# Eight PSUM banks dealt out anew in a kernel of two attentions and a mixture of experts

## The chip, the cores and the metric

The kernel runs on one core of one Trainium2 chip. The metric is the device time of one execution in microseconds (us). A core has five engines that run side by side, each through a queue of its own in fixed order: TensorE (PE, matmuls; its weight loads are shown apart as PEld), VectorE (DVE), ScalarE (ACT), GpSimd (POOL) and SyncE (SP), which here only issues DMAs. Matmuls write to PSUM, which has eight banks of 128 partitions x 512 fp32 numbers; DVE and ACT read the results from there.

## The reference, cut to what matters

The input x has 16 sequences of 256 tokens with 128 channels, all fp32. Four blocks follow each other, each with a layernorm ahead of it and its result added to x:

```
x = x + attention_a(layernorm(x))   # 16 heads of 8, in blocks of 64 tokens
x = x + ffn(layernorm(x))           # 8 experts, hidden 512, the best 2 per token
x = x + attention_b(layernorm(x))   # 16 heads of 8, across the 16 sequences, with a bias
x = x + ffn(layernorm(x))           # the same experts again

scores = einsum(q, k) * scale (+ bias);  attn = softmax(scores);  out = einsum(attn, v)
g = x @ Wg[e];  u = x @ Wu[e];  h = silu(g) * u;  y = (h @ Wd[e]) / sqrt(12)
out = y of the two chosen experts, weighted by the softmax of their two logits
```

## The kernel before, in words

The tokens are cut into four quarters (64 positions of all 16 sequences), each quarter into two halves, each half into four groups of 128 tokens. x stays in SBUF.

**First attention** (`prepare_a`, `attention_a`, layer 0). For each half `prepare_a` normalizes, transposes (product lnp), and makes keys and queries (products k and q). Queries are copied out of their bank by four ACT instructions (line 313). Then for each group: a product v for the values (line 339), two score tiles sc, one for each block of 64 tokens (line 396); DVE takes the maximum over keys (line 404) and subtracts it (line 405), which is the last reading of the score bank; ACT takes exp of both tiles in one instruction (line 410); PE transposes them in two products t (line 415), which ACT copies (line 419); PE multiplies with the values into the product o (line 426), which DVE divides (lines 356, 358).

**Second attention** (`normal_b`, `prepare_b`, `attention_b`, `finish_b`, layer 1). It has the same steps, with one score tile for each group (line 503), read once by DVE, which adds the bias (line 510); the output is transposed once more (product ot, line 481) and projected (product y_B, line 560).

**Router** (`router`, `tile_tables`). After each quarter it normalizes again, computes logits (product lg, line 585) and ranks (line 648 waits for a copy by POOL), and writes the rows by indirect DMA, sorted by expert. It runs beside the next quarter.

**Experts** (`experts`). Each of the two layers has 39 tiles of 256 rows. A tile is fetched with its expert's three weights by SP's DMAs, turned (product xt, line 875, copied by ACT in line 877), and worked on in two pairs of hidden chunks. A pair computes gate g and up u into one bank each (line 933, 128 x 512); ACT takes tanh of g (line 938), DVE multiplies with g again (line 939, the last reading of g) and with u (line 941, the only reading of u). The down product acc collects both pairs (line 883); ACT copies it (line 891), PE turns it back (product y, line 894), ACT scales it (line 899) and POOL writes the rows out by indirect DMA (line 906). The down matmuls of one pair are written behind gate and up of the next.

**Order.** `weave` and `run` at the end write the order of the work: the generators of attention, preparation, router and expert units are stepped in fixed ratios. No expert work stands beside the first three quarters of the first attention; about half of what layer 0's first lists hold is put beside the fourth, and the later units run beside the second attention. A planner in the framework then fixes each engine's queue, starting from that order, and says which bank each tile gets; on the chip an instruction waits for the last reader of the tile that held its bank before.

**PSUM.** Four pools hold the eight banks: `ps_gu` (tag gu) has three, for g and u; `ps_acc` one, for acc; `ps_sc` (tag sc) two, for the scores of both attentions (lines 393 and 500); `ps_mm` (tag mm) two, for every product called small here (function `psum`: lnp, k, q, v, t, o, xt, y, ot, y_B, lg, rank, count).

Of the kernel before, what the change touches and what calls it, by code (L numbers as in the profile page):

```python
# [10 lines left out]
F32 = mybir.dt.float32  # L11
# [6 lines left out]
PSUM = bass.MemoryType.PSUM  # L18

P = 128  # L20
# [90 lines left out]
def hybrid_kernel(  # L111
# [24 lines left out]
    p6 = ctx.enter_context(tc.tile_pool(name="p6", bufs=6))  # L136
    p3 = ctx.enter_context(tc.tile_pool(name="p3", bufs=3))
    dram = ctx.enter_context(tc.tile_pool(name="dram", bufs=1, space=bass.MemoryType.DRAM))
    ps_gu = ctx.enter_context(tc.tile_pool(name="ps_gu", bufs=3, space=PSUM))
    ps_acc = ctx.enter_context(tc.tile_pool(name="ps_acc", bufs=1, space=PSUM))  # L140
    ps_sc = ctx.enter_context(tc.tile_pool(name="ps_sc", bufs=2, space=PSUM))
    ps_mm = ctx.enter_context(tc.tile_pool(name="ps_mm", bufs=2, space=PSUM))


    xq = [const.tile([P, NG, C], F32, name=f"xq{q}") for q in range(NQ)]
# [110 lines left out]
    def psum(name):  # L256
        return ps_mm.tile([P, 512], F32, tag="mm", name=name)
# [95 lines left out]
    def divided(o, name):  # L353
        o = o.rearrange("p (h d) -> p h d", d=D + 1)
        rec = p2.tile([P, H], F32, tag="rec", name=f"rec_{name}")
        nc.vector.reciprocal(rec, o[:, :, D])
        att = p2.tile([P, H, D], F32, tag="att", name=f"att_{name}")
        att_last[0] = nc.vector.tensor_tensor(  # L358
            att, o[:, :, 0:D], rec.unsqueeze(2).to_broadcast([P, H, D]), ALU.mult
        ).ins  # L360
        return att.rearrange("p h d -> p (h d)")
# [20 lines left out]
    def attention_a(q, half):  # L382
        lnT, qT, kx = ready.pop((q, half))
        for g in range(4 * half, 4 * half + 4):
            n = f"A{q}_{g}"
            vt = va[g % 2]
            values(vt, lnT, g % 4, 2, wv_sb, n)
            yield


            ex = p2.tile([P, 2, 8, BS], F32, tag="ex", name=f"ex_{n}")
            for b in range(2):
                sc = ps_sc.tile([P, 512], F32, tag="sc", name=f"sc_{n}_{b}")
                blk = 2 * (g % 4) + b
                for v in range(2):
                    nc.tensor.matmul(  # L396
                        sc[:, v * 4 * BS : (v + 1) * 4 * BS],
                        lhsT=qT[:, blk, 2 * v : 2 * v + 2, :].rearrange("p r k -> p (r k)"),
                        rhs=kx[:, :, blk * BS : (blk + 1) * BS],
                        start=True, stop=True,  # L400
                    )
                sc3 = sc.rearrange("p (h k) -> p h k", k=BS)
                mx = p3.tile([P, 16], F32, tag="mx", name=f"mx_{n}_{b}")
                nc.vector.tensor_reduce(mx[:, 0:8], sc3, AX.X, ALU.max)  # L404
                beat[0] = nc.vector.tensor_tensor(  # L405
                    ex[:, b], sc3, mx[:, 0:8].unsqueeze(2).to_broadcast([P, 8, BS]),
                    ALU.subtract,
                ).ins
                yield
            beat[0] = nc.scalar.activation(ex, ex, AF.Exp).ins  # L410
            eT = p2.tile([P, 2, 4, P], F32, tag="eT", name=f"eT_{n}")
            for b in range(2):
                pt = psum(f"t_{n}_{b}")
                for i in range(4):
                    nc.tensor.transpose(  # L415
                        pt[:, i * P : (i + 1) * P],
                        ex[:, b, 2 * i : 2 * i + 2, :].rearrange("p h k -> p (h k)"), ident,
                    )
                nc.scalar.copy(eT[:, b].rearrange("p a b -> p (a b)"), pt)  # L419
                yield  # L420
            po = psum(f"o_{n}")
            for b in range(2):
                for i in range(8):

                    u, v = i // 2 % 2, i // 4
                    nc.tensor.matmul(  # L426
                        po[b * BS : (b + 1) * BS, i * 18 : (i + 1) * 18],
                        lhsT=eT[:, b, 2 * v + i % 2, u * BS : (u + 1) * BS],
                        rhs=vt[:, b, 2 * i : 2 * i + 2, :].rearrange("p h d -> p (h d)"),
                        start=True, stop=True,  # L430
                    )
            att = divided(po[:, 0 : H * (D + 1)], n)
            beat[0] = att_last[0]
            nc.gpsimd.tensor_tensor(att, att, bv_bc, ALU.add)  # L434
            nc.gpsimd.tensor_tensor(xq[q][:, g, :], xq[q][:, g, :], att, ALU.add)
            yield
# [36 lines left out]
    def attention_b(q, half):  # L473
        xt, qT, kx = ready.pop((q, half))
        if half == 0:
            outs[q] = p1.tile([P, S, BS], F32, tag="oT", name=f"oT_{q}")
        oT = outs[q]

        def turn(g, att):
            pot = psum(f"ot_B{q}_{g}")  # L480
            nc.tensor.transpose(pot[:, 0:P], att, ident)
            nc.scalar.activation(
                oT.rearrange("c s t -> c t s")[:, 8 * g : 8 * g + 8, :],
                pot[:, 0:P].rearrange("c (t s) -> c t s", s=S),
                AF.Identity, bias=b_sb[:, B_IV : B_IV + 1],
            )

        pending = None
        for dg in range(2 * half, 2 * half + 2):
            for gg in range(2):  # L490
                g = 2 * dg + gg
                values(vb[gg], xt, g % 4, 4, wi_sb[:, 2 * P : 3 * P], f"B{q}_{g}")
                yield


            ex = p2.tile([P, 2, H, 32], F32, tag="ex", name=f"ex_B{q}_{dg}")
            for gg in range(2):
                g = 2 * dg + gg
                n = f"B{q}_{dg}_{gg}"
                sc = ps_sc.tile([P, 512], F32, tag="sc", name=f"sc_{n}")  # L500
                for j in range(4):
                    blk = 4 * (g % 4) + j
                    nc.tensor.matmul(  # L503
                        sc[:, j * P : (j + 1) * P],
                        lhsT=qT[:, blk].rearrange("p r k -> p (r k)"),
                        rhs=kx[:, :, blk * 32 : (blk + 1) * 32],
                        start=True, stop=True,
                    )
                sb = p2.tile([P, H, 32], F32, tag="sb", name=f"sb_{n}")
                nc.vector.tensor_tensor(  # L510
                    sb, sc.rearrange("p (h k) -> p h k", k=32),
                    pair_bias.unsqueeze(1).to_broadcast([P, H, 32]), ALU.add,
                )
                yield
                mx = p3.tile([P, 16], F32, tag="mx", name=f"mx_{n}")
                nc.vector.tensor_reduce(mx, sb, AX.X, ALU.max)
                beat[0] = nc.vector.tensor_tensor(
                    ex[:, gg], sb, mx.unsqueeze(2).to_broadcast([P, H, 32]), ALU.subtract
                ).ins
                yield  # L520
            nc.scalar.activation(ex, ex, AF.Exp)
            for gg in range(2):
                g = 2 * dg + gg
                n = f"B{q}_{g}"
                pt = psum(f"t_{n}")
                for j in range(4):
                    nc.tensor.transpose(  # L527
                        pt[:, j * P : (j + 1) * P],
                        ex[:, gg, 4 * j : 4 * j + 4, :].rearrange("p h k -> p (h k)"),
                        ident,  # L530
                    )
                eT = p2.tile([P, 2, 4, P], F32, tag="eT", name=f"eT_{n}")
                nc.scalar.copy(eT[:, 0].rearrange("p a b -> p (a b)"), pt)
                yield
                if pending is not None:
                    turn(*pending)
                po = psum(f"o_{n}")
                for j in range(4):
                    for r in range(4):
                        nc.tensor.matmul(  # L540
                            po[32 * j : 32 * (j + 1), r * 36 : (r + 1) * 36],
                            lhsT=eT[:, 0, j, 32 * r : 32 * (r + 1)],
                            rhs=vb[gg][:, j, 4 * r : 4 * r + 4, :].rearrange(
                                "p h d -> p (h d)"
                            ),
                            start=True, stop=True,
                        )
                pending = g, divided(po[:, 0 : H * (D + 1)], n)
                beat[0] = att_last[0]
                yield  # L550
        turn(*pending)
        yield
# [476 lines left out]
    for layer in range(2):  # L1029
# [10 lines left out]
        for q in range(NQ):  # L1040
            for half in range(2):
# [20 lines left out]
                if layer == 1 and half == 1:  # L1062
                    finish_b(q)
                    if q == NQ - 2:
                        n = BEGIN_B - 3
# [53 lines left out]
```

## Time and profile before

| | |
|---|---|
| three runs, us | 1083.53, 1084.24, 1073.32 (median 1083.53) |
| profiled execution, us | 1007.37 |
| its span from the first to the last instruction, us | 1005.3 |
| mean granted TensorE clock in it | 0.923 |
| PE, PEld, DVE, ACT, POOL busy, share of the span | 88%, 72%, 62%, 39%, 37% |
| HBM traffic | 106 GB/s over the span |
| first attention alone / with experts | 20 to 233 us / 233 to 345 us |
| experts of layer 0 alone | 345 to 455 us |
| second attention with experts | 455 to 830 us |
| experts of layer 1 alone, and the end | 830 to 1005 us |

The profile is one execution recorded by the hardware. Its page begins with the busy time of each engine, then cuts the span into 40 equal slices (a digit is the busy share in tenths; PEclk is the clock that PE was granted, in tenths of full speed). A row of waits reads: the instruction that stood, what released it, us in total, times, longest. A row of the timeline reads: start, duration, engine, line, operation, what is written from what, shapes, count, and in brackets the idle time of the engine ahead of it and its releaser. A row of a stage table reads: stretch, its length, busy us of PE, PEld, DVE, ACT and POOL with their counts of instructions, PE's clock, the share of the DMA engines, GB/s. Releasers are inferred from semaphore events. Ends of matmuls are modelled, so a busy PE is not PE at its peak.

### The profile page before, as it was taken

How to read it: one execution, taken by the hardware profiler on the slowest of the kernel's cores; microseconds unless marked ns; L12 is line 12 of the kernel's file. 1: busy time of each engine (PE TensorE's matmuls, PEld its weight loads, DVE VectorE, ACT ScalarE, POOL GpSimd, SP SyncE). 2: the span in 40 equal slices, each digit the busy share in tenths (PEclk: the TensorE clock that was granted, in tenths of full speed). 3: DMA queues.
4: the chain of work that ended last, by engine and by line, in shares of the span. 5: the costliest groups of instructions: out<-in, count | busy, mean ns of one | idle time of the engine just before them, and what ended most of it. 6: DMA issues, size and time to landing. Idle time of an engine off the chain costs nothing.

```text
span 1005.3 us, 17682 instructions
## 1 busy us (share of the span) xinstructions
PE 880.1 (88%) x5992; PEld 723.8 (72%) x5992; DVE 623.4 (62%) x1741; ACT 395.9 (39%) x773; POOL 371.3 (37%) x460
## 2 busy tenths in 40 slices
PE   3988698888999999989987989797988999998993
PEld 1776577665878888877766777585767787886882
DVE  5666555665576685559657665674867685555542
ACT  2443333233353434335543345352534333443431
POOL 2112442261165375337001362163516457332322
PEclk9998776798999999999978699799999999999997
DMA  7000000013133476675110122025403456668762
GB/s 192 19 2 1 17 29 1 9 41 105 44 109 112 126 207 208 191 229 169 44 64 22 43 87 67 20 81 174 127 10 110 138 148 193 198 181 271 225 192 83
DMA packets 104922, 107.69 MB, mean 107 GB/s; under 512 B 10688, under 2 KB 80320, under 8 KB 104832
## 3 DMA queue, kind: packets, MB, share of 16 engines
q1 hardware_dynamic: 95024, 87.36, 29.8%
q0 software_dynamic: 9088, 18.89, 5.4%
q8 instruction: 48, 0.79, 0.3%
q10 hardware_dynamic: 720, 0.30, 0.1%
q14 instruction: 42, 0.34, 0.1%
HBM read 83.38 MB, written 23.13 MB: 106 GB/s over the span
## 4 chain that ended last, share of the span: by engine, by line
PE 65%; DVE 13%; DMA 6%; ACT 5%; POOL 5%; issue 4%; SPq 1%; ACTq 0%; POOLq 0%; DVEq 0%
PE g L933 11%; PE u L933 10%; PE acc L883 10%; PE o_A L426 5%; PE sc_A L396 4%; PE v_B L339 4%; PE o_B L540 3%; PE t_A L415 3%; PE sc_B L503 2%; DMA back<-results 2%; DMA results<-yo,to 2%; PE t_B L527 2%; DMA xin<-sorted_in 2%; PE lg_F L585 2%; POOL sorted_in L680 2%
## 5 line engine op out<-in xcount | busy, mean ns | idle before, releaser
L906 POOL DMA_INDIRECT results<-yo,to x156 | 153.3, 982 | 235.8 <-ACT yo L899 203.5
L883 PE MATMUL acc<-h,w 128*128 128x256 f32 x624 | 167.0, 388 | 2.8 <-DVE h L941 2.5
L933 PE MATMUL u<-xT,w 128*128 128x256 f32 x624 | 163.8, 384 | 5.4 <-DVE th L939 5.2
L933 PE MATMUL g<-xT,w 128*128 128x256 f32 x624 | 166.4, 386 | 0.5 <-ACT xT L877 0.5
L938 ACT ACTIVATE th<-g 128x512 f32<-128x512 f32 x156 | 93.4, 599 | 162.2 <-PE g L933 159.8
L939 DVE SCALAR_TENSOR_TENSOR th<-th,g 128x512 f32<-128x512 f32 x156 | 106.1, 681 | 74.9 <-ACT th L938 73.7
L680 POOL DMA_INDIRECT sorted_in<-rows,pos_i_F x128 | 126.0, 985 | 66.6 <-issue 25.2
L883 PEld LDWEIGHTS acc<-h,w 128*128 128x128 f32 x624 | 117.1, 193 | 24.2 <-DVE h L941 5.9
L933 PEld LDWEIGHTS g<-xT,w 128*128 128x128 f32 x624 | 116.6, 193 | 17.4 <-issue 1.9
L933 PEld LDWEIGHTS u<-xT,w 128*128 128x128 f32 x624 | 113.1, 192 | 21.2 <-DVE th L939 7.6
L941 DVE TENSOR_TENSOR h<-th,u 128x512 f32<-128x512 f32 x156 | 106.3, 682 | 11.7 <-PE u L933 1.9
L396 PE MATMUL sc_A<-k_A,q_A 128*128 128x256 f32 x256 | 81.5, 448 | 27.7 <-DVE ex_A L405 18.4
L396 PEld LDWEIGHTS sc_A<-k_A,q_A 128*128 128x128 f32 x256 | 51.7, 223 | 41.2 <-issue 21.3
L426 PEld LDWEIGHTS o_A<-va,eT_A 128*64 128x64 f32 x1024 | 60.7, 147 | 11.2 <-ACT eT_A L419 7.6
L891 ACT COPY yT<-acc 128x256 f32<-128x256 f32 x78 | 29.3, 375 | 99.5 <-PE acc L883 99.4
L426 PE MATMUL o_A<-va,eT_A 128*64 128x18 f32 x1024 | 64.1, 219 | 1.0 <-ACT eT_A L419 0.9
L899 ACT ACTIVATE yo<-y,xin 128x128 f32<-128x128 f32 x156 | 48.4, 365 | 36.0 <-PE y L894 36.0
L434 POOL TENSOR_TENSOR att_A<-att_A,bv_bc 128x128 f32<-128x128 f32 x32 | 14.6, 455 | 129.0 <-DVE att_A L358 123.2
L419 ACT COPY eT_A<-t_A 128x512 f32<-128x512 f32 x64 | 36.0, 587 | 45.6 <-PE t_A L415 45.4
L404 DVE TENSOR_REDUCE mx_A<-sc_A 128x8 f32<-128x512 f32 x64 | 43.2, 684 | 14.9 <-PE sc_A L396 14.6
L410 ACT ACTIVATE ex_A<-ex_A 128x1024 f32<-128x1024 f32 x32 | 33.9, 1059 | 38.4 <-DVE ex_A L405 32.0
L415 PEld LDWEIGHTS t_A<-k_sb,ex_A 128*128 128x128 f32 x256 | 34.4, 159 | 18.2 <-ACT ex_A L410 6.7
(173 smaller groups left out, 1326.8 us busy)
## 6 DMA issues: line engine op xcount, KB each, us to landing
w<-in_wg SPq DMA_DIRECT2D x78, 256.0 KB, 2.8
w<-in_wu SPq DMA_DIRECT2D x78, 256.0 KB, 3.5
w<-in_wd SPq DMA_DIRECT2D x78, 256.0 KB, 3.9
xin<-sorted_in SPq DMA_DIRECT2D x78, 132.0 KB, 2.1
back<-results SPq DMA_DIRECT2D x16, 512.0 KB, 4.6
results<-yo,to POOLq DMA_INDIRECT x156, 3.7
sorted_in<-zero SPq DMA_DIRECT2D x2, 1056.0 KB
sorted_in<-rows,pos_i_F POOLq DMA_INDIRECT x128, 2.3
```

The source lines that it names most:

```text
L396: nc.tensor.matmul(sc[:, v * 4 * BS : (v + 1) * 4 * BS], lhsT=qT[:, blk, 2 * v : 2 * v + 2, :].rearrange("p r k -> p (r k)"), rhs=kx[:, :, ...
L404: nc.vector.tensor_reduce(mx[:, 0:8], sc3, AX.X, ALU.max)
L415: nc.tensor.transpose(pt[:, i * P : (i + 1) * P], ex[:, b, 2 * i : 2 * i + 2, :].rearrange("p h k -> p (h k)"), ident,)
L426: nc.tensor.matmul(po[b * BS : (b + 1) * BS, i * 18 : (i + 1) * 18], lhsT=eT[:, b, 2 * v + i % 2, u * BS : (u + 1) * BS], rhs=vt[:, b, 2 * ...
L680: put_row = nc.gpsimd.indirect_dma_start(out=sorted_in[layer], out_offset=bass.IndirectOffsetOnAxis(ap=pos_i[:, k, g : g + 1], axis=0), in ...
L883: nc.tensor.matmul(acc[:, 0:TT], lhsT=w[:, 2, hc * P : (hc + 1) * P], rhs=h[:, j * TT : (j + 1) * TT], start=(hc == 0), stop=(hc == NHC - 1),)
L899: nc.scalar.activation(y[:, b, :], py[:, b * P : (b + 1) * P], AF.Identity, scale=t[:, b, C : C + 1],)
L906: put_row = nc.gpsimd.indirect_dma_start(out=results[layer], out_offset=bass.IndirectOffsetOnAxis(ap=to[:, b : b + 1], axis=0), in_=y[:, b ...
L933: nc.tensor.matmul(p[:, j * TT : (j + 1) * TT], lhsT=w[:, k, hs], rhs=xT, start=True, stop=True,)
L938: nc.scalar.activation(th, pg, AF.Tanh, scale=0.5)
L939: nc.vector.scalar_tensor_tensor(th, th, 1.0, pg, ALU.add, ALU.mult)
L941: beat[0] = nc.vector.tensor_tensor(h, th, pu, ALU.mult).ins
```

## The change

The pool of the scores is gone. Scores of both attentions are now tiles of the pool and the tag of gate and up, which has four banks instead of three; the pool of the small products has three instead of two; acc keeps its one. The sum is eight as before. Nothing else is edited.

```diff
-    ps_gu = ctx.enter_context(tc.tile_pool(name="ps_gu", bufs=3, space=PSUM))
+    ps_gu = ctx.enter_context(tc.tile_pool(name="ps_gu", bufs=4, space=PSUM))
     ps_acc = ctx.enter_context(tc.tile_pool(name="ps_acc", bufs=1, space=PSUM))
-    ps_sc = ctx.enter_context(tc.tile_pool(name="ps_sc", bufs=2, space=PSUM))
-    ps_mm = ctx.enter_context(tc.tile_pool(name="ps_mm", bufs=2, space=PSUM))
+    ps_mm = ctx.enter_context(tc.tile_pool(name="ps_mm", bufs=3, space=PSUM))
...
-                sc = ps_sc.tile([P, 512], F32, tag="sc", name=f"sc_{n}_{b}")
+                sc = ps_gu.tile([P, 512], F32, tag="gu", name=f"sc_{n}_{b}")
...
-                sc = ps_sc.tile([P, 512], F32, tag="sc", name=f"sc_{n}")
+                sc = ps_gu.tile([P, 512], F32, tag="gu", name=f"sc_{n}")
```

## The prediction

> **What bounds the kernel now.** I read the engine totals first, then the slices, the stage table, TensorE's waits with their idle stretches, and last the timeline around the longest of them.
>
> ```profile
> PE 880.1 (88%) x5992; PEld 723.8 (72%) x5992; DVE 623.4 (62%) x1741; ACT 395.9 (39%) x773; POOL 371.3 (37%) x460
> PE   3988698888999999989987989797988999998993
> PEclk9998776798999999999978699799999999999997
> ```
>
> TensorE (PE) is busy for 880 of 1005 us; no other engine passes 62%. Its clock row falls below 9 in two stretches, and these are the attention stages. The stage table, with busy us per engine and the granted clock after the engines:
>
> ```profile
> 20.00:233.00 213.00, 179.09 (x1356) 142.70 (x1356) 130.53 (x405) 79.25 (x113) 65.63 (x95) 0.84 0.10 31
> 233.00:345.00 112.00, 105.17 (x723) 87.57 (x723) 71.80 (x201) 46.43 (x91) 45.74 (x57) 0.97 0.29 88
> 345.00:455.00 110.00, 107.01 (x525) 93.13 (x525) 70.42 (x182) 43.14 (x111) 53.68 (x58) 0.98 0.67 204
> 455.00:770.00 315.00, 274.06 (x2229) 218.66 (x2228) 210.66 (x614) 136.26 (x240) 106.68 (x126) 0.91 0.24 74
> ```
>
> 20 to 233 us is the first attention alone: PE idles 34 us at clock 0.84. From 233 expert tiles fill its gaps, 345 to 455 is experts alone (97% busy), and from 455 to 770 the second attention is mixed with experts: PE idles 41 us. So a PE wait removed before 233 us reaches the end: nearly full PE work follows. What PE waits for there:
>
> ```profile
> PE sc_A L396 <- DVE ex_A L405: 18.4, 7, 3.5
> PE sc_A L396 <- ACT q_A L313: 7.2, 11, 1.1
> PE rank_F L648 <- POOL taken_F L632: 7.0, 2, 3.5
> PE t_A L415 <- ACT ex_A L410: 2.5, 3, 0.9
> ```
>
> The first row is a bank wait: score matmuls need nothing from the subtraction of line 405 but a free score bank, and there are two. The others are data waits, which banks don't touch. It comes once near the start of a half (seven of eight). The one at 79 us:
>
> ```profile
> 77.59 1.13 PE L396 MATMUL sc_A<-k_A,q_A 128*128 128x256 f32 x4 [0.21 <-ACT q_A L313]
> ...
> 80.20 1.27 DVE L404 TENSOR_REDUCE mx_A<-sc_A 128x8 f32<-128x512 f32 x2
> 81.40 1.27 DVE L405 TENSOR_TENSOR ex_A<-sc_A,mx_A 128x512 f32<-128x512 f32 x2
> 82.22 3.04 PE L396 MATMUL sc_A<-k_A,q_A 128*128 128x256 f32 x8 [3.50 <-DVE ex_A L405]
> ...
> 82.77 1.06 ACT L410 ACTIVATE ex_A<-ex_A 128x1024 f32<-128x1024 f32 x1 [5.23 <-DVE ex_A L405]
> ...
> 85.05 1.69 PE L415 MATMUL t_A<-k_sb,ex_A 128*128 128x128 f32 x8
> ```
>
> Two score tiles are done at 78.7; VectorE (DVE), busy normalizing for the router, frees the first at 82.1; PE then computes the next group's two tiles, and because its queue is in order the transposes wait behind them until 85.05, though exp ended at 83.83. In the second attention the same mixture has waits on small-product banks:
>
> ```profile
> PE v_B L339 <- ACT q_B L313: 6.3, 4, 2.8
> PE u L933 <- DVE th L939: 5.2, 8, 1.4
> PE sc_B L503 <- DVE sb_B L510: 3.5, 3, 2.8
> ```
>
> **What the Trainium skill says.** *Perfetto Trace Analysis*, Optimization Strategy: the same gap repeating on the engine that should be saturated can mean too little PSUM for the next tile. The trace agrees: seven gaps of 1.6 to 3.5 us at one line. The same page, Matmuls: independent groups should rotate through different banks so that evacuation overlaps the next matmuls. Before 233 us the trace shows three of eight banks (gate/up) unused. *TensorE: Matmul & The Clock Gate*, Part 1, says that an idle window of about 3.4 us halves the clock. The windows agree in kind: after the gap at 79 us the clock reads 0.50 from 83 to 86 us and 1.00 from 87.
>
> **The change part by part.** No instruction or DMA is added or removed; each matmul and reader stays. Only which bank a tile waits for changes, and with it the order in the queues, since a planner orders them and hands out the banks (in the trace, from 26.8 us, half a score tile stands between a group's transposes and its output matmuls, which the code doesn't write there).
>
> (a) Scores, first attention alone: two banks become four. Tiles three and four can follow tile two at once; they take 1.97 to 3.75 us and would end before exp does (78.7 + 3.0 = 81.7 against 83.83). The next limit is exp, which depends on DVE. The gain is therefore not the wait but the distance from the end of exp to the first transpose: 0.26, 0.19, 1.22, 1.94, 1.94, 1.76, 1.87, together 9.2 us over the seven places. In the first two it is a bare handover of 0.2 us, which stays: 9.2 - 7 x 0.2 = 7.8 us. Lower end 0, if DVE ends last anyway; upper end 18.2, the seven idle stretches whole.
>
> (b) Clock. 0.84 over 213 us is 34 us of clock lost, 68 us at half rate. Score work moved into the gap raises PE's activity in five late gaps that are followed by half rate; a half-rate period of 3.4 us costs 1.7, so 8.5 for five. Much half rate follows groups of small matmuls, not gaps, so I take 5. Ends: 0 and 15.
>
> (c) Small products, three banks for two. The value product waits 2.8 us behind the four query activations; with a third bank one of its two tiles (1.1 us) goes ahead, but scores still need the queries. Half of 6.3: 3.1 us. PE's other waits of one small product for the reader of another (transposes, logits, layernorm, row 0.2 to 0.8 each) sum to 4.7; half: 2.3. Ends 0 and 11.
>
> (d) Gate and up: a fourth bank removes the wait of u for the reading of an older gate, 5.2 us; down then waits for h from the same DVE, so I take half, 2.5. Ends 0 and 5.
>
> (e) The price: from 233 to 345 and 455 to 830, gate, up and scores had 3 + 2 banks and have 4. A queued u or score then waits for the oldest reader, always DVE; behind it on PE's queue stand down, transposes and output matmuls, for which ACT and DVE wait in turn. No row shows this wait. Nearest is the score wait of 2.8 us, in the ten halves where both live (two first, eight second): 0 to 28 us. Occupancy speaks for the low end: per group of some 14.6 us, two score tiles of some 3 us and four gate/up tiles of some 4 us (from matmul to last reader, read off the timeline) fill 22 of 58 bank-us. I take 0.3 us a half: 3.
>
> (f) Down keeps its one bank: 0. What covers it is the order of pairs: only 0.5 us of waits of y for the copy of line 891 is seen; without cover that copy costs 0.38 us a tile, 29 over 78.
>
> Sum: 7.8 + 5 + 3.1 + 2.3 + 2.5 - 3 = 17.7 us. The profiled span of 1005.3 becomes 987.6 (its own time, 1007.4, becomes 989.7). The median is 1083.5, 76 us above that execution, and the page doesn't say where they lie; I assume the same stalls and take the same microseconds off: 1065.8, say **1066 us**.
>
> **Rivals.** *Forecast, chance 0.42*: 1066, own range 1056 to 1075. *The wait only moves, 0.25*: DVE's chain (normalizing, maximum, subtraction, exp) ends last, the scores come early and PE stands at the transposes instead. For it: in the first two gaps the distance is only 0.2, and PE waits for exp already. Against: 1.2 to 1.9 in the other five. It leaves some 4 us: 1080. *The clock recovers, 0.15*: gaps below the threshold keep the rate up also later; (b) gives 15, (a) 10, the rest 10: 1083.5 - 35 = 1048. For it: the clock row; against: half rate also where PE is 100% busy. *The shared ring binds, 0.18, slower*: on the mixed stages PE's order runs ahead of DVE, which is at 64 to 74% there, and u or scores stand for DVE. Price 28 us over ten halves, with only 12 gained elsewhere: 1083.5 + 16 = 1099. It decides from 20.7 us of ring waits on (3 + 17.7), 2 us a half. Against it: occupancy, and only 0.2 us of u-waits in 233 to 345. That the change does nothing at all would end where the moved wait ends and is counted there.
>
> **How the numbers follow.** Under 1% this measurement tells nothing from no change (the three runs span 1%), so faster means under 1072.7, slower over 1094.4. Faster: 0.37 of the forecast's 0.42 and all of the clock case: 0.52. Same: 0.05 of the forecast, 0.22 of the moved wait, 0.03 of a weak ring: 0.30. Slower: 0.15 of the ring, 0.03 of a moved wait with a worse order: 0.18. The range 1040 to 1094 leaves out about 0.18 above and a little below.
>
> **What would show it.** In the changed profile the row of scores waiting for line 405 should fall from 18.4 to under 3, the clock of the first attention rise from 0.84 to about 0.88, and 20 to 233 us shorten by some 13. v_B waiting for q_B should halve. New u or score waits on DVE in the mixed stages should sum to a few us. If transposes wait for exp by 10 us more, the second rival holds; if ring waits pass 20 us, the last. An order of queues that puts router or expert work ahead of attention would make all of this wrong.

## The result and the profile after

| | us |
|---|---|
| changed kernel, median of 20 runs | 1084.46 (1078.27 to 1087.78) |
| kernel before beside it, median of 20 runs | 1078.53 (1066.33 to 1087.26) |
| ratio, with its 95% interval | 1.0083 (1.0062 to 1.0105) |
| profiled span of the changed kernel | 1083.7 |

The forecast was 1066, a gain. The changed kernel is 0.8% slower instead: less than the 1% under which the forecast called two times the same, but the interval leaves out both no change and any gain.

One thing must be known before two profiles are compared. The runs fell on chips of two levels: on some the kernel before takes about 1003 us, on others about 1075, and its other versions move along. The profile that the prediction read is of the first level, the profile of the changed kernel of the second. So I compare only inside a level, with a second profile of each kernel.

The changed kernel's page, busy time of the engines, and the clock row of the slices:

```profile
PE 909.0 (84%) x5992; PEld 751.6 (69%) x5992; DVE 619.6 (57%) x1741; ACT 396.7 (37%) x773; POOL 371.0 (34%) x460
...
PEclk9878677776899999998998869988988998999997
```

PE is still the busiest. The digits 6 to 8 of the clock row at the left, the first attention, have become more, not fewer. The stage table says it inside one level and for the same piece of work, the first six halves of the first attention, which have no expert work beside them (columns: stretch, length, PE, PEld, DVE, ACT, POOL busy, clock, DMA share, GB/s). The kernel before, on a 1075-us chip:

```profile
20.00:245.00 225.00, 183.48 (x1356) 146.45 (x1356) 130.31 (x406) 79.38 (x113) 65.87 (x95) 0.83 0.09 29
```

The changed kernel, on a chip of the same level:

```profile
20.00:263.00 243.00, 199.40 (x1350) 162.69 (x1350) 124.39 (x400) 79.42 (x114) 65.23 (x93) 0.76 0.10 30
```

18 us more for the same matmuls (the counts agree within the records that a trace loses), at clock 0.76 instead of 0.83. Of the 18 us, 15.9 are in PE's busy time and only 2.1 in its idle time: the same matmuls run longer, and a list of waits can't show that. PE's waits in the changed kernel:

```profile
PE sc_A L395 <- DVE ex_A L404: 17.8, 6, 3.9
...
PE t_A L414 <- ACT ex_A L409: 14.7, 7, 6.6
...
PE v_B L338 <- DVE vb L344: 3.3, 4, 0.9
...
PE u L932 <- DVE sb_B L509: 1.3, 1, 1.3
...
PE g L932 <- DVE th L938: 0.7, 1, 0.7
```

The first row is the wait that four banks were to remove: 18.4 us in the prediction's profile and 19.9 in the second one, 17.8 now. The second has grown (5.4 in the second profile of the kernel before). The last two are new waits in the ring of gate, up and scores; with 1.7 us of sc_B behind sb_B (3.5 before) they are all that the ring makes PE wait for in the mixed stages. The row of v_B behind q_B, 6.3 before, is gone.

Where the time went, by the first and last instruction of each stage in single traces (us):

| stage | 1075-us chips: before | changed (two traces) | 1003-us chips: before | changed |
|---|---|---|---|---|
| first attention, first sc to last o | 326.7 | 350.1, 347.7 | 310.9 | 327.3 |
| experts of layer 0 alone | 145.5 | 148.6, 143.5 | 133.4 | 132.3 |
| second attention, first xt_B to last o_B | 349.5 | 340.0, 339.5 | 321.6 | 308.8 |
| from there to the end | 228.2 | 225.2, 226.2 | 218.9 | 212.4 |

On both levels the change does two opposite things: the first attention loses 16 to 23 us, and the second attention and the end win 12 to 19. What is gained lies in the other stages, not in the one where the forecast put most of it. The small sum is what is left of two larger amounts of opposite sign.

**What became of the wait.** The start of a half in the changed kernel's timeline (start, duration, engine, line, what, shapes, count, idle time ahead of it):

```profile
128.31 1.13 PE L310 MATMUL q_A<-lnT_A,wq_sb 128*128 128x512 f32 x2
...
129.37 1.11 PE L425 MATMUL o_A<-va,eT_A 128*64 128x18 f32 x16
...
130.98 3.72 PE L395 MATMUL sc_A<-k_A,q_A 128*128 128x256 f32 x16
...
137.75 1.28 DVE L404 TENSOR_TENSOR ex_A<-sc_A,mx_A 128x512 f32<-128x512 f32 x2
...
138.58 2.48 PE L395 MATMUL sc_A<-k_A,q_A 128*128 128x256 f32 x8 [3.88 <-DVE ex_A L404]
...
140.85 1.92 PE L414 MATMUL t_A<-k_sb,ex_A 128*128 128x128 f32 x8
```

The sixteen score matmuls from 130.98 to 134.70 are four tiles, in four banks, without a stop. But behind them in PE's queue stand not the transposes but the scores of a third group, tiles five and six, and tile five needs the bank of tile one. So PE stands 3.88 us for the same subtraction at line 404, one group later. Exp (line 409) runs from 139.12 to 140.18; the transposes begin at 140.85, behind tiles five and six, and at half speed: 1.92 us, where they take 1.04 at full clock. This fits what the Trainium skill says (*TensorE: Matmul & The Clock Gate*, Part 1: an idle window of some 3.4 us halves the clock): the granted clock reads 0.50 from 140 to 143 us.

The six tiles stand ahead of the first transposes in the first six of the eight halves; before, it was four. PE's queue, as compiled, for the second half of the first quarter (x2: two matmuls; sc_4_0 is the first block's tile of group 4; x16 and x8: 16 or 8 output matmuls, which the trace shows as 32 and 16):

```
before   sc_4_0 sc_4_1 sc_4_0 sc_4_1 sc_5_0 x2 sc_5_1 x2 | t_4 | sc_6_0 o_4 x16 v_5 sc_6_0 sc_6_1 | t_5 | sc_6_1 o_5 x16 v_6 sc_7_0 x2 lnp sc_7_1 x2 | t_6 | o_6 x16 v_7 k | t_7 | o_7 x16 q v
changed  sc_4_0 sc_4_1 sc_5_0 sc_5_1 sc_4_0 sc_4_1 sc_5_0 sc_5_1 sc_6_0 x2 sc_6_1 x2 | t_4 | sc_7_0 o_4 x16 v_5 sc_7_0 | t_5_0 sc_7_1 t_5_1 | o_5 x8 v_6 o_5 x8 lnp sc_7_1 | t_6 | o_6 x8 v_7 o_6 x8 v_7 k | t_7 | o_7 x8 q o_7 x8 v
```

Three things differ: the first four tiles are interleaved, the third group stands ahead of the first transposes, and the outputs of a group are cut in two with a product v or q between the halves (at 128.31 above it is q). Of the 32 groups, 30 have their outputs in one piece before, 12 in the changed kernel.

### The profile page after: what moved, and what is told of

Its sections match the earlier page's. It is cut to its first block, busy times and chain, and to the rows that moved or that the text cites. A ratio compares the mean times of both kernels' runs of the same rounds, so it can differ in the third digit from the quotient of the medians.

```text
span 1083.7 us, 17683 instructions
## 1 busy us (share of the span) xinstructions
PE 909.0 (84%) x5992; PEld 751.6 (69%) x5992; DVE 619.6 (57%) x1741; ACT 396.7 (37%) x773; POOL 371.0 (34%) x460
## 4 chain that ended last, share of the span: by engine, by line
PE 63%; DVE 13%; DMA 6%; issue 6%; another core or an unknown queue 4%; ACT 4%; POOL 3%; SPq 1%; ACTq 0%; POOLq 0%; DVEq 0%
PE acc L882 10%; PE g L932 10%; PE u L932 10%; PE o_A L425 7%; PE sc_A L395 3%; PE t_A L414 3%; PE o_B L539 2%; PE v_B L338 2%; PE v_A L338 2%; PE sc_B L502 2%; DMA xin<-sorted_in 2%; DMA back<-results 2%; PE lg_F L584 1%; PE t_B L526 1%
## 5 line engine op out<-in xcount | busy, mean ns | idle before, releaser
L932 PE MATMUL g<-xT,w 128*128 128x256 f32 x624 | 168.8, 391 | 3.3 <-issue 2.3
L932 PE MATMUL u<-xT,w 128*128 128x256 f32 x624 | 167.2, 388 | 2.1 <-DVE sb_B L509 1.3
L932 PEld LDWEIGHTS g<-xT,w 128*128 128x128 f32 x624 | 118.9, 197 | 21.5 <-issue 4.7
L932 PEld LDWEIGHTS u<-xT,w 128*128 128x128 f32 x624 | 115.6, 195 | 18.0 <-issue 2.7
L395 PE MATMUL sc_A<-k_A,q_A 128*128 128x256 f32 x256 | 77.2, 436 | 18.9 <-DVE ex_A L404 17.8
L425 PEld LDWEIGHTS o_A<-va,eT_A 128*64 128x64 f32 x1024 | 72.8, 158 | 18.2 <-issue 10.2
L425 PE MATMUL o_A<-va,eT_A 128*64 128x18 f32 x1024 | 78.2, 227 | 1.1 <-ACT eT_A L418 1.0
L414 PE MATMUL t_A<-k_sb,ex_A 128*128 128x128 f32 x256 | 49.2, 345 | 24.6 <-ACT ex_A L409 14.7
L414 PEld LDWEIGHTS t_A<-k_sb,ex_A 128*128 128x128 f32 x256 | 41.7, 185 | 40.1 <-ACT ex_A L409 18.5
L355 DVE RECIPROCAL rec_A<-o_A 128x16 f32<-128x16 f32 x32 | 8.2, 258 | 104.5 <-PE o_A L425 73.2
L898 ACT ACTIVATE yo<-y,xin 128x128 f32<-128x128 f32 x156 | 48.4, 365 | 17.3 <-PE y L893 11.1
```

What stands on the lines that cost most here:

```text
L395: nc.tensor.matmul(sc[:, v * 4 * BS : (v + 1) * 4 * BS], lhsT=qT[:, blk, 2 * v : 2 * v + 2, :].rearrange("p r k -> p (r k)"), rhs=kx[:, :, ...
L414: nc.tensor.transpose(pt[:, i * P : (i + 1) * P], ex[:, b, 2 * i : 2 * i + 2, :].rearrange("p h k -> p (h k)"), ident,)
L425: nc.tensor.matmul(po[b * BS : (b + 1) * BS, i * 18 : (i + 1) * 18], lhsT=eT[:, b, 2 * v + i % 2, u * BS : (u + 1) * BS], rhs=vt[:, b, 2 * ...
L898: nc.scalar.activation(y[:, b, :], py[:, b * P : (b + 1) * P], AF.Identity, scale=t[:, b, C : C + 1],)
L932: nc.tensor.matmul(p[:, j * TT : (j + 1) * TT], lhsT=w[:, k, hs], rhs=xT, start=True, stop=True,)
```

## The experiments

Times are medians beside the kernel before on the same chip; "first" and "second" are the lengths of the two attentions in the trace.

| kernel | small / gate, up / scores banks | ratio (95%) | first | second |
|---|---|---|---|---|
| *1075-us chips:* before, second profile | 2 / 3 / 2 | | 326.7 | 349.5 |
| five shared banks, two small | 2 / 5 shared | 1.0096 (1.0059 to 1.0132) | 328.2 | 365.3 |
| three small, none shared | 3 / 2 / 2 | 1.001 (0.9981 to 1.004) | 327.8 | 342.6 |
| changed, scores two groups ahead | 3 / 4 shared | 1.003 (1.0 to 1.0059) | 348.8 | 336.6 |
| before, outputs cut | 2 / 3 / 2 | 1.0064 (1.0036 to 1.0092) | 329.5 | 355.1 |
| scores three of their own | 2 / 2 / 3 | 1.01 (1.0051 to 1.0149) | 326.9 | 355.1 |
| changed, again | 3 / 4 shared | 1.0031 (1.0007 to 1.0054) | 347.7 | 339.5 |
| changed, v, k and q behind the outputs | 3 / 4 shared | 0.975 (0.9697 to 0.9803) | 315.8 | 338.1 |
| *1003-us chips:* before, first profile | 2 / 3 / 2 | | 310.9 | 321.6 |
| changed, v, k and q behind the outputs | 3 / 4 shared | 0.9733 (0.9702 to 0.9764) | 297.7 | 306.3 |
| changed, v and k behind them | 3 / 4 shared | 0.9783 (0.9746 to 0.982) | 302.5 | 308.1 |
| changed, q behind them | 3 / 4 shared | 0.9858 (0.9825 to 0.9892) | 319.2 | 308.2 |
| changed, v, k, q behind, scores two groups ahead | 3 / 4 shared | 0.9898 (0.9858 to 0.9937) | 314.9 | 307.7 |
| three small, none shared, v, k, q behind | 3 / 2 / 2 | 0.9789 (0.9749 to 0.983) | 302.9 | 295.8 |
| changed, second profile | 3 / 4 shared | one run: 1002.65 beside 1003.37 | 327.3 | 308.8 |

**A second profile of the kernel before.** No edit.

> The kernel before, unchanged, profiled a second time. Theory of an odd profile: the profiled execution that the prediction was read from (span 1005.3 us, clock 0.923) is 7% below that kernel's own median of 1078.5, so it was not an ordinary one; this profile shows a span of 1070 to 1082 and a clock of 0.88 to 0.90, with TensorE stretches in the first attention that the first profile does not have. Rival: the profile repeats at 1005 and timed executions are slower than profiled ones for another reason.

It took 1071.8 us with a span of 1069.8. The wait of scores stays (19.9 us, 7 times), so the stalls that the prediction read are those of ordinary executions; only the level differs.

**Five banks shared, two small ones.**

```diff
-    ps_gu = ... bufs=3    ps_sc = ... bufs=2    ps_mm = ... bufs=2
+    ps_gu = ... bufs=5    (scores in it)        ps_mm = ... bufs=2
```

> One part alone: scores share the ring of gate and up, which keeps all five banks that the two pools had; small products keep two. Run-ahead theory (the planner spends every bank it gets on scores of a later group, and the wait for a score bank comes back one or more groups later): the waits of scores for line 404/405 in the first attention still sum to 15 us or more, and the time is that of the change, ratio to before 1.00 to 1.01. Rival, a ring of four is too short beside the experts: with five the time falls to or below before, ratio 0.98 to 1.00. Rival, the third small bank costs the time: this kernel has two, so ratio 1.00.

Slower by 1%, as the run-ahead theory had it, but not for its reason: it expected a wait of 15 us or more. The scores' wait is nearly gone here (2.5 us), with scores of three groups and more ahead of the first transposes, and the first attention isn't shorter: 328.2 against 326.7. A wait removed from PE's list was worth nothing. The outputs are together (30 of 32). The loss lies in the second attention, where the waits in the ring sum to only 2 us; what costs it is open.

**Three small banks, none shared.**

```diff
-    ps_gu = ... bufs=3    ps_mm = ... bufs=2
+    ps_gu = ... bufs=2    ps_mm = ... bufs=3
```

> The other part alone: small products get three banks, scores keep their own two, gate and up go down to two. Rival theory that the third small bank costs the time (output matmuls of a group are split around the next value product in TensorE's queue): ratio 1.005 to 1.02. Run-ahead theory: the first attention is like before, and only gate and up with two banks cost something in the expert stages, 5 to 20 us, with waits of g and u for DVE that sum to that.

No difference. The second attention wins 7 us, the end loses 5, and the first attention stands still although 16 of the 32 outputs are cut. So the third small bank is what cuts the outputs (30, 30 and 29 whole groups in the kernels with two small banks, 12 to 16 in those with three), and cutting by itself isn't the loss of 21 to 23 us.

**Scores at most two groups ahead.** In the changed kernel the first scores of group g stand behind the transposes of group g-2 in PE's queue, by a dependency that only orders the queue and waits for nothing:

```diff
+                    if len(turned_a) > 1:
+                        tc.add_manual_dep(mm.ins, turned_a[-2].name, NOSYNC, ...)
```

> The changed kernel with one order written down: in the first attention the scores of a group stand in TensorE's queue behind the transposes of the group two before, so that four score tiles may run ahead but no more. Run-ahead theory: the waits of scores for the subtraction fall from 17.8 us to under 4, transposes start as exp ends, and the time falls 8 to 15 us below the change, ratio to before 0.99 to 1.00. Rival, VectorE's chain ends last anyway: the wait moves to the transposes and the time stays within 3 us of the change.

The wait of scores is gone and has moved whole. PE's waits in this kernel:

```profile
PE t_A L420 <- ACT ex_A L415: 38.0, 11, 6.6
```

38.0 us against 14.7 in the changed kernel; the first attention keeps its 349 us. So taking the third group back isn't worth anything while the outputs stay cut (16 of 32 whole), and the third group isn't what loses the first attention.

**v, k and q behind the outputs.** In the changed kernel every v, k and q product is ordered behind the outputs of the group before it, again without a wait. In the kernel before, this dependency moves no instruction in any queue. (`o_last` holds the last output product of each group.)

```diff
+    def behind_o(mm):
+        if o_last:
+            tc.add_manual_dep(mm.ins, o_last[-1].name, NOSYNC, ...)
...
-        nc.tensor.matmul(pq, lhsT=w, rhs=src, start=True, stop=True)
+        behind_o(nc.tensor.matmul(pq, lhsT=w, rhs=src, start=True, stop=True))
```

and the same for k and v.

> The changed kernel, in which the v, k and q products stand behind all output products of the group before them in TensorE's queue (a dependency without a wait). The queue it gives also puts the transposes of a group ahead of the third group's scores, as before the change, so that in the first attention it is nearly the queue of the kernel before with the changed banks. Theory (the new banks let the planner reorder TensorE's queue, and the reordered queue is what costs): the first attention, from the first scores to the last o_A, comes back from 350 us to about 328, the second attention keeps its 340, and the time falls to about 1062 (1055 to 1070). Rival (the shared banks themselves cost, expert tiles and scores wait for each other's ring): the first attention stays at 345 or more and the time within 5 us of 1084. Third (each is half of it): 1072 to 1076.

975.75 us where the kernel before takes 1003.37 and the changed kernel, in a single run, 1002.65. The expectation describes the queue wrongly: the interleaving and the third group ahead of the transposes are in it as in the changed kernel. What is different is the place of v, k and q: 24 of 32 groups have their outputs whole. So it isn't the scores' order alone that loses the first attention. Once more, on a 1075-us chip:

> The changed kernel with v, k and q behind the outputs, once more, beside the changed kernel on one chip. If its gain is its queue's, it holds on another chip or at another time: ratio 0.968 to 0.980 to the kernel before. If it was that chip's, the ratio comes nearer to 1 than 0.985.

0.975: the gain doesn't depend on the chip. The same place as above in this kernel:

```profile
110.52 1.83 PE L432 MATMUL o_A<-va,eT_A 128*64 128x18 f32 x32 [0.29 <-ACT eT_A L425]
...
112.28 1.12 PE L317 MATMUL q_A<-lnT_A,wq_sb 128*128 128x512 f32 x2
...
114.94 3.72 PE L402 MATMUL sc_A<-k_A,q_A 128*128 128x256 f32 x16 [1.09 <-ACT q_A L319]
...
120.46 1.97 PE L402 MATMUL sc_A<-k_A,q_A 128*128 128x256 f32 x8 [1.80 <-DVE ex_A L411]
...
122.26 1.04 PE L421 MATMUL t_A<-k_sb,ex_A 128*128 128x128 f32 x8
```

Again x16 and x8, six tiles, stand ahead of the transposes. From the end of the last outputs (112.35 here, 130.48 there) to the third group's scores it is 8.1 us in both: division, two additions on POOL, normalizing for the router, maximum, subtraction. But here q is still to be done in that time, so PE stands 1.80 us at the end of it instead of 3.88, and runs on at full clock. The stage table of this kernel:

```profile
20.00:231.00 211.00, 170.49 (x1357) 142.34 (x1358) 125.50 (x409) 78.95 (x115) 65.86 (x96) 0.86 0.09 28
```

The same six halves take 211 us at clock 0.86 (243 at 0.76 in the changed kernel, 225 at 0.83 before). Of the 32 us that come back, 28.9 are PE's busy time.

**Which product between the halves?** q alone behind the outputs, and v and k alone; in both, 18 of the 32 groups have whole outputs.

> The changed kernel with only the q product ordered behind the outputs, so that the last group of a half has its outputs in one piece; v still cuts those of other groups, and the scores of the third group stay ahead of the first transposes. Theory (what costs is the product between the halves of a half's last outputs: from these hangs the chain division, two additions, router's normalizing, maximum, some 6 us in every kernel, that starts the next half): most of the gain of the kernel with q, k and v ordered comes back, ratio 0.978 to 0.990, first attention shorter by 15 to 25 us than the changed kernel's (about 327 or 349 us by the chip). Rival (each cut costs the same, whatever group): about half, 0.987 to 0.993, and the same for the kernel with v and k ordered.

> The changed kernel with only v and k ordered behind the outputs; q still stands between the halves of the last group's outputs, in as many groups as v cuts in the other kernel. Theory (the last group's cut costs): little comes back, ratio 0.993 to 1.003, first attention within 10 us of the changed kernel's. Rival (each cut costs the same): 0.987 to 0.993.

It is the other way round. Of the 29.6 us between 327.3 and 297.7, v and k alone bring 24.8 (302.5), q alone 8.1 (319.2). The intervals of the two times don't touch. My theory of the last group falls, and so does the rival of equal cuts. PE's waits, in the kernel with q ordered:

```profile
PE t_A L421 <- ACT ex_A L416: 12.7, 7, 4.9
...
PE sc_A L402 <- DVE ex_A L411: 7.8, 6, 2.2
```

and in the kernel with v and k ordered:

```profile
PE sc_A L402 <- DVE ex_A L411: 17.7, 6, 3.9
...
PE t_A L421 <- ACT ex_A L416: 7.9, 3, 6.6
```

The kernel with the long wait of scores is the faster one, 17 us shorter in this stage. The row on which the prediction rested doesn't measure a loss. What differs most is the speed of the matmuls. The first six halves on 1003-us chips, the changed kernel and then the one with v and k ordered:

```profile
20.00:246.00 226.00, 188.88 (x1357) 154.86 (x1358) 125.00 (x404) 80.57 (x115) 65.31 (x94) 0.81 0.11 33
20.00:222.00 202.00, 169.28 (x1358) 139.60 (x1359) 125.47 (x405) 79.72 (x115) 65.06 (x94) 0.88 0.09 28
```

Of the 24 us between them, 19.6 are PE's busy time. The stops for the subtraction are the same in both (18.0 and 17.7 us, longest 3.9), so it isn't their length that makes the clock differ.

In a half whose outputs run at full clock in both traces, I read where the changed kernel loses against the one with v and k ordered. The changed kernel, on a 1003-us chip:

```profile
66.64 1.11 PE L425 MATMUL o_A<-va,eT_A 128*64 128x18 f32 x16
67.68 0.71 PE L338 MATMUL v_A<-wv_sb,lnT_A 128*128 128x128 f32 x4
68.32 1.11 PE L425 MATMUL o_A<-va,eT_A 128*64 128x18 f32 x16
...
69.85 0.60 PE L395 MATMUL sc_A<-k_A,q_A 128*128 128x256 f32 x2
72.08 1.09 PE L414 MATMUL t_A<-k_sb,ex_A 128*128 128x128 f32 x8 [1.62 <-ACT ex_A L409]
```

With v and k ordered:

```profile
58.77 1.11 PE L432 MATMUL o_A<-va,eT_A 128*64 128x18 f32 x16
59.81 0.70 PE L402 MATMUL sc_A<-k_A,q_A 128*128 128x256 f32 x2
60.44 1.11 PE L432 MATMUL o_A<-va,eT_A 128*64 128x18 f32 x16
61.48 0.71 PE L345 MATMUL v_A<-wv_sb,lnT_A 128*128 128x128 f32 x4
...
62.80 1.06 PE L421 MATMUL t_A<-k_sb,ex_A 128*128 128x128 f32 x8 [0.17 <-DVE va L351]
```

It is v that moved: where v stood between the output halves, the half's last score matmul stands now. (The two moves come together, and no run separates them.) From these outputs to the next transposes it is 5.44 us in the changed kernel and 4.03 here, with the 1.62 us for exp gone. Of the 3.6 us that this half differs by (30.8 against 27.2), 1.4 lie here, 0.5 in what follows (the next group's outputs are cut in the changed kernel and whole here), and 1.7 ahead of the first outputs, where the clock reads 0.50 from 58 to 61 us in the changed kernel and 1.00 in the other.

**Both orders by hand.** Outputs together and scores two groups ahead:

> The same dependency on top of the kernel whose scores stand at most two groups ahead. If the split outputs are the loss that was left there, the first attention falls from 349 us to about 328 and the time from 1077 to about 1060. If the loss was the transposes that wait for the exp (38 us in that row), nothing but a few us changes: 1072 to 1077, and the row stays above 25 us.

0.9898, and transposes wait 31.1 us for exp (15 times). The row stays, as the second expectation has it, and the stage falls nearly as in the first: with the outputs cut it was 22 us longer than in the kernel before, and it is 4 us longer here (314.9 against 310.9). Against the kernel with v, k and q ordered alone it is 17 us longer (314.9 against 297.7). With scores held back to two groups PE stands at the transposes instead, and loses: the third group ahead is a gain, not the fault.

**v, k and q behind the outputs, nothing shared.** The dependency on the kernel with three small banks:

> The kernel with three banks for small products and two for gate and up, scores in their own two, with the same dependency: no shared ring. Its first attention was 328 us with the outputs split, so the theory expects little there; time 1068 to 1076. If split outputs cost everywhere by themselves (32 groups, some 0.4 to 0.8 us each), the time falls by 13 to 25 us, to 1050 to 1062.

0.9789, or 22.5 us: the second figure, not the theory's. But only 8 us of it lie in the first attention. With this order the third small bank is worth 2.1%, the bank that gate and up lost for it included; the shared ring adds at most a little (0.9733 against 0.9789, the intervals overlap). Most of it lies in the second attention (295.8 against 321.6), where the queue is that of the kernel without the dependency, which won only 7 us there on a 1075-us chip; why the levels differ so is open.

**The changed kernel, a second profile.**

> The changed kernel once more, unchanged, for a second trace. If the stages of one execution are steady, the first attention takes 350 us within 4 and the second 340 within 4. If they vary as the first profile of the kernel before did (311 us in the first attention against 327 in a later one), stage differences of 10 us between single traces mean little.

The stages follow the level of the chip, and on one level they are steady: 327.3 and 308.8 us here, 350.1 and 340.0 in the first profile, and 347.7 and 339.5 in the next, which is of that level again:

> The changed kernel as it is, beside the others on one chip. Theory: 0 to 1% above the kernel before, as in its first comparison (1.0083).

1.0031 (1.0007 to 1.0054), below the first comparison's 1.0083.

**Outputs cut in the kernel before.** In 24 of 32 groups the next v is put between the output halves:

```diff
+                if b == 1 and g % 4 < 3:
+                    values(va[(g + 1) % 2], lnT, g % 4 + 1, 2, wv_sb, f"A{q}_{g + 1}")
...
+                        tc.add_manual_dep(mm.ins, v_mm[0].ins.name, NOSYNC, ...)
```

> The kernel before, banks unchanged, with one thing added: the v products of the next group are put between the two halves of a group's output products in 24 of the 32 groups of the first attention, as the changed kernel's queue has them. Theory (splitting the halves costs by itself): two runs of 16 output products take 1.11 us each against 1.83 us for 32 together, so 0.4 us a group at full clock and 0.65 at half (1.90 twice against 3.13): 10 to 16 us in the first attention, time 0.8 to 1.6% above the kernel before. Rival (the halves are split where TensorE waits anyway, and the loss is in the scores' order): within 0.3% of the kernel before.

Slower by 0.64%, between the two expectations, and only 3 us of it lie in the first attention: in the old queue a v between the halves costs little.

**A third bank for the scores alone.** The prediction's first step by itself:

```diff
-    ps_gu = ... bufs=3    ps_sc = ... bufs=2
+    ps_gu = ... bufs=2    ps_sc = ... bufs=3
```

> The kernel before with one bank moved from gate and up to the scores: scores three of their own, gate and up two, small products two; nothing is shared and the outputs stay together (35 rows in TensorE's queue against 34). It is the prediction's first step alone. The prediction's step (a scores bank more takes the wait of scores for the subtraction away): the row of scores behind the subtraction falls from 18 us to under 8, the first attention by 4 to 8 us, and the time by up to 8, less what the two banks for gate and up cost. Theory (TensorE's queue runs scores of a further group ahead with every bank, and the wait moves to the transposes): the first attention stays within 4 us of the kernel before, transposes behind the exp rise by about what the scores' row falls, and the time is 0 to 1% above.

The first attention stays (326.9). PE's waits:

```profile
PE g L933 <- DVE th L939: 24.5, 12, 4.2
PE sc_A L396 <- DVE ex_A L405: 15.1, 7, 3.1
```

The row of scores falls by a few us only; the queue here runs one tile of the third group ahead, as the bank allows. The 1% goes with two banks for gate and up: g waits 24.5 us for the older gate's reading, which the kernel before's list doesn't show, and the end, which has no scores, takes 241 us instead of 228.

## Why the prediction was wrong, point by point

**Step (a), scores, -7.8.** The step that failed is "Tiles three and four can follow tile two at once ... The next limit is exp". It kept the queue of the kernel before and added banks to it, though the prediction itself had noted that a planner orders the queues. With four banks the planner puts six tiles, not four, ahead of the transposes, and the bank wait is back one group later (17.8 us of 18.4). And the wait was no measure: from the last outputs to the scores that the subtraction releases it is 8.1 us with a stop of 3.88 us and with one of 1.80. (One of the seven waits, 3.5 us at 240 us, doesn't lie before 233 us, where the step put them all.)

The distance that the step did price, from the end of exp to the first transpose, summed over eight halves, went from 9.7 to 9.9 us on one level and from 11.1 to 8.3 on the other: +0.2 and -2.8. Nor is this distance a gain by itself. It fell from 11.1 to 1.6 us with five shared banks and to 0.4 with scores two groups ahead, and the first attention was 1.5 and 22 us longer than before. With v, k and q ordered both fall (the distance to 3.4 and 1.4), but with three small banks, none shared, and the same order, the stage is 8 us shorter at a distance of 9.1.

**What the sum had no term for.** From the first transposes to the last outputs of a half, over eight halves, the changed kernel takes 242.8 us for 225.0 on one level and 267.2 for 239.9 on the other; with v, k and q ordered 216.9 and 238.1. These 18 to 27 us are the loss. Shown: it goes with the places of v and k in PE's queue (24.8 of 29.6 us), places which the planner gives them with three small banks (12 to 16 whole groups, against 29 and 30 with two). Shown too: most of it is PE's busy time, the same matmuls at a lower clock (19.6 of 24 us in the first six halves). Not shown: why these places lower the clock, and why they cost so much here. In the two kernels without the shared ring, cut outputs cost +1.1 and +2.8 us; with the ring, on the same level, the stage is 21 to 23 us longer with scores three groups ahead and 22 with two, so the third group isn't the reason.

**Step (b), clock, -5.** Predicted was 0.84 to 0.88. It went from 0.83 to 0.76 on one level and from 0.84 to 0.81 on the other. With v, k and q ordered it is 0.86 and 0.88, which is the forecast's figure, but not by its mechanism, score work that fills the stops. With v and k ordered the stops are as long as in the changed kernel (17.7 us) at clock 0.88; with q ordered they are 7.8 us at clock 0.79. The clock doesn't follow them.

**Step (c), third small bank, -5.4; step (d), fourth gate/up bank, -2.5.** Their rows behaved as predicted. On the 1003-us chips v_B behind q_B went from 6.3 to nothing, and 3.2 us of v_B behind vb took their place (a wait for the DVE instruction that reads an older v product out of its bank): 3.1 net, the predicted figure. u behind th went from 5.2 to nothing. But the stage won 12.8 us there and 9.5 to 10.0 on the other chip, where (c), (d) and (e) together came to 4.9: the terms were too small by half. What the rest is made of wasn't isolated.

**Step (e), shared ring, +3.** u behind sb_B 1.3 and g behind th 0.7 make 2.0 us. The rival in which the ring binds (28 us) is excluded by these rows, and by the second attention, which became shorter.

**Rivals.** The "moved wait" came nearest, 1080 us with transposes behind exp up by 10; measured were 1084 and +9.3 (5.4 to 14.7). That the time is so near is luck, for it is the sum of a loss and a gain that this rival doesn't have. Its mechanism is half right: the transposes do stand longer, but the wait of scores didn't move to them, it stayed. The forecast's last sentence named a bad order of queues as what would make all wrong, and looked for it in the wrong work, router and experts; it was attention's own.

**The base.** Taking the stalls from an execution 76 us under its median did no harm: the row agrees on both levels (18.4 and 19.9 us).

## What to carry to other kernels

More PSUM banks don't only end waits: where a planner orders the queues they also change the order, of other products too. So compare the compiled queues first, and try the new banks with the harmful move undone by ordering-only dependencies; here that turned +0.3 to +0.8% into -2.5 to -2.7% (on a 1003-us chip the changed kernel has a single run, level with the kernel before). And a long row of waits on an engine isn't a loss if the chain that it waits for is as long without it. Compare the length of the stage, and in it PE's busy time and clock, before a wait or a distance is given a price.

## What the runs showed of the hardware that was not expected

The same changed kernel had a span of 1000.8 us in one profile and of 1083.7 and 1076.9 in two others, and whole comparisons move with it (the kernel before: 1003 and 1005, or 1072 and 1078). One chip gave the upper level at two times, and another the lower level between them. In each profile of the upper level six to eleven stretches of 1.5 to 5.4 us between 120 and 950 us, 19 to 29 us in all, have PE, its weight loads, DVE and ACT standing together, mostly at the same places of the program (147.2 to 150.1 in the changed kernel is one); in those of the lower level there is none. What ends them the trace doesn't tell, and they are only a third of the difference; this stays open.

32 output matmuls in one piece take 1.83 us, two pieces of 16 take 1.11 each; at half clock 3.20 against 1.90 each. The rows overlap: at full clock the next product starts 1.76 us after the whole begins and 1.04 us after a piece, so that two pieces hold PE for 2.08 us.
